# The last norm of a mixture-of-experts block: transposes after scaling replaced by products with a diagonal of the norm's weight, the mean by row products, and the idle products before the experts moved to rows of x

## The chip, the cores and the metric

The kernel runs on one core of one Trainium2 chip. The metric is the device time of one launch in microseconds; where several runs are given it is their median. A profile is one execution taken by the hardware profiler; its span runs from the first to the last instruction of the program, and its own time is a little longer. All numbers are float32 unless a line says otherwise.

## The reference

The reference is one layer over 625 nodes with 768 channels: a graph attention part, a linear attention part, and then a feed-forward part with two global norms and a mixture of experts. Only the last part is touched. With `x` the residual rows:

```
a = attn(ln(x));  h = layernorm_global(a + ln(x), ln1_w, ln1_b)
m = sum over the two best experts k of  vals[k] * (gelu(h @ fc_w[k] + fc_b[k]) @ proj_w[k] + proj_b[k])
out = x + layernorm_global(m + h, ln2_w, ln2_b)

layernorm_global(z, w, b) = (z - mean(z)) / sqrt(var(z, ddof=1) + 1e-12) * w + b
```

In `layernorm_global` mean and variance are taken over all 625 x 768 numbers; `w` and `b` have one number for each channel. The experts are chosen once for all nodes, from the mean of the router's scores.

## The kernel before, in words

**Layout.** The residual `xs` is held in rows: 5 tiles of 125 nodes (`TP`), 768 channels along the free axis. The feed-forward part works in channel-major tiles: 6 tiles (`NC`) of 128 channels (`P`), 625 nodes along the free axis. `hT` is the sum before the first norm, `x3` the normed input of the experts, `zT` the sum `m + h` before the last norm, all three channel-major. `bcol` holds bias and norm vectors by channel, in columns; `LN2W` and `LN2B` are the columns where the last norm's weight and bias begin.

**Order of the work.** A scheduler of the language orders each engine's instructions by data dependence and program order, except in blocks marked `manual_schedule`, where the named engines take program order. Semaphores between engines, and waits for memory that is used again, are put in by the language. SyncE's queue issues the weights' loads; GpSimd's queue issues loads that broadcast a vector to all partitions.

**Before the experts (L1058 to L1092).** `global_norm` (L1007) makes the mean and the factor of the first norm: statistics on VectorE, one product with `mean_w` (128 x 128, all 1/128, L1002) that gives the mean over partitions, and a power on GpSimd (L1019). `scale_bias` (L1024) turns them into a scale and a bias for each channel, and `x3` is written from `hT`. Beside this TensorE does nine products that nobody reads (L1064, `psidle`), of `mean_w` with 313 columns of `hT`. Then the memory of `hT` is given back (`fms.close()`), and the pool `ep` of the experts is opened in its place: weights `wq`, input sums `xt`, hidden tiles `h` and `t`, temporaries.

**The experts (L1219 to L1255).** A product of two matrices is done with seven half-size products in place of eight (`seven`, L1128): sums of quarter blocks of the weights (`quarter_sums` L1118, `last_sum` L1123) and of the inputs (`xt`, L1207 to L1211), all on VectorE, then seven products into four PSUM banks `al`, `be`, `ga`, `de`, and sums of the banks on VectorE (L1149 to L1162), with one copy on ScalarE (L1146). The loops run over two experts `k`, two groups `u0` of 6 pairs of hidden blocks, then over the hidden blocks `f` (first matrix, activation on ScalarE at L1234) and over three pairs of output blocks `c` (second matrix). An output quarter `q` is added to `zT` with the expert's gate (L1248); in the last group each finished half tile of `zT` is measured as well (L1251, into `st2`).

**The tail (L1262 to L1279).** `global_norm` and `scale_bias` run again for the last norm. Then `zT` is scaled in place, three channel tiles on ScalarE (L1266) and three on VectorE (L1269). For each of the five row tiles, six transposes (L1274) bring it into two PSUM banks, one VectorE add (L1277) adds `xs`, and two stores on SyncE's queue (`move_rows`, L73: rows 0 to 111 and 112 to 124) write it out. Three buffers `fin` are in use.

Of the kernel before, what the change touches and what calls it, by code (L numbers as in the profile page):

```python
# [8 lines left out]
F32 = mybir.dt.float32  # L9
# [4 lines left out]
AF = mybir.ActivationFunctionType  # L14
OP = mybir.AluOpType
# [24 lines left out]
def kernel(ctx: ExitStack, tc: tile.TileContext, a: dict, out: bass.AP):  # L40
# [1020 lines left out]
        nc.tensor.matmul(ps_r[0:1, 0:NEXP], chan[:, k, 0:1], rww[:, k, :], start=(k == 0), stop=(k == NC - 1))  # L1061

    ps_w = b1("psidle")
    for i in range(9):  # L1064
        nc.tensor.matmul(ps_w[:, 0:NH2], mean_w, hT[:, i % NC, 0:NH2], start=True, stop=True)
    att.close()


# [27 lines left out]
    pse_.close()  # L1096
    moe = ExitStack()
    ep = moe.enter_context(tc.tile_pool(name="ep", bufs=1, reuse_waits="tile"))
    psq = moe.enter_context(tc.tile_pool(name="psq", bufs=8, space=PSUM, reuse_waits="tile"))

# [22 lines left out]

    A11, A12, S1, A22, S2, S3, S4 = range(7)

    def seven(name, ws, b):  # L1128


        def product(ps, s, blk, first):
            n = 3 * len(ws)
            for k in range(n):
                nc.tensor.matmul(ps[:, 0:NH2], ws[k // 3][:, s, k % 3, :], b[blk](k),  # L1134
                                 start=(first and k == 0), stop=(k == n - 1), skip_group_check=True)

        def bank(nm):
            return psq.tile([P, BANK], F32, tag="q", name=f"{nm}_{name}")

        def tmp(nm):  # L1140
            return ep.tile([P, NH2], F32, tag=nm, name=f"{nm}_{name}", bufs=2)

        al, be, ga, de = bank("al"), bank("be"), bank("ga"), bank("de")
        product(al, A11, "11", True)
        p1 = tmp("p1")
        nc.scalar.copy(p1, al[:, 0:NH2])  # L1146
        product(be, S2, "t2", True)
        u = tmp("u")
        nc.vector.tensor_add(u, be[:, 0:NH2], p1)  # L1149
        product(ga, S1, "t1", True)  # L1150
        p5 = tmp("p5")
        nc.vector.tensor_add(p5, ga[:, 0:NH2], u)
        product(de, S3, "t3", True)
        c22 = tmp("c22")
        nc.vector.tensor_sub(c22, de[:, 0:NH2], p5)  # L1155
        product(al, A12, "21", False)
        product(ga, S4, "22", False)
        c12 = tmp("c12")
        nc.vector.tensor_add(c12, ga[:, 0:NH2], u)
        product(de, A22, "t4", False)  # L1160
        c21 = tmp("c21")
        nc.vector.tensor_sub(c21, de[:, 0:NH2], u)  # L1162
        return al[:, 0:NH2], c12, c21, c22
# [10 lines left out]


    def gates():
        ones = mp.tile([1, P], F32, name="ones")
        nc.vector.memset(ones, 1.0)
        lm = mp.tile([1, 1], F32, name="lm")
        nc.vector.tensor_scalar_mul(lm, top[:, 0:1], -1.0)  # L1180
        ls = mp.tile([1, 1], F32, name="ls")
        nc.scalar.activation(lg, lg, AF.Exp, bias=lm, accum_out=ls)
        nc.scalar.activation(top[:, 0:2], top[:, 0:2], AF.Exp, bias=lm)
        nc.vector.reciprocal(ls, ls)
        nc.vector.tensor_scalar_mul(top[:, 0:2], top[:, 0:2], ls)
        ps = psq.tile([P, BANK], F32, tag="q", name="pstv")
        nc.tensor.matmul(ps[:, 0:2], ones, top[:, 0:2], start=True, stop=True)
        vals = mp.tile([P, 2], F32, name="vals")
        nc.vector.tensor_copy(vals, ps[:, 0:2])
        ebc = []  # L1190
        for k in range(2):
            er = mp.tile([NF + NC, P], F32, tag="er", name=f"er{k}", bufs=2)
            nc.sync.dma_start(er[0:NF, :], a["L0_ffn_fc_b"][bass.ds(ex[k], 1), :].rearrange("e (f p) -> (e f) p", p=P))
            nc.sync.dma_start(er[NF:, :], a["L0_ffn_proj_b"][bass.ds(ex[k], 1), :].rearrange("e (f p) -> (e f) p", p=P))
            ps = psq.tile([P, BANK], F32, tag="q", name=f"pser{k}")
            nc.tensor.transpose(ps[:, 0:NF + NC], er, ident[0:NF + NC, 0:NF + NC])
            ec = mp.tile([P, NF + NC], F32, tag="ec", name=f"ec{k}", bufs=2)
            nc.vector.tensor_copy(ec, ps[:, 0:NF + NC])
            ebc.append(ec)
        pbias = mp.tile([P, NC], F32, name="pbias")  # L1200
        nc.vector.tensor_scalar_mul(pbias, ebc[0][:, NF:], vals[:, 0:1])
        nc.vector.scalar_tensor_tensor(pbias, ebc[1][:, NF:], vals[:, 1:2], pbias, op0=OP.mult, op1=OP.add)
        return vals, ebc, pbias
# [12 lines left out]
          "t3": lambda k: xt[:, 2, k, :], "t4": lambda k: xt[:, 3, k, :]}  # L1216

    st2 = const.tile([P, 2 * NC, 6], F32, name="st2")
    GU = 6  # L1219
    for k in range(2):  # L1220
        prw = a["L0_ffn_proj_w"][bass.ds(ex[k], 1), :, :].rearrange("e (f p) c -> p (e f) c", p=P)
        for u0 in range(0, HF, GU):
            hb = []
            for f in range(u0, u0 + GU):
                w, w_next = w_next or fc_weights(k, f), None
                cs = seven(f"f{k}_{f}", [w], bx)
                if k == 0 and f == 0:
                    vals, ebc, pbias = gates()
                    for c in range(NC):
                        nc.scalar.activation(zT[:, c, :], x3[:, c, 0:N], AF.Identity, bias=pbias[:, c:c + 1])  # L1230
                h = [ep.tile([P, NH2], F32, tag=f"h{q}", name=f"h{q}_{k}_{f}", bufs=GU + 2) for q in range(4)]
                for q in range(4):
                    fb = f + HF * (q // 2)
                    nc.scalar.activation(h[q], cs[q], AF.Gelu_apprx_tanh, bias=ebc[k][:, fb:fb + 1])  # L1234
                t = [ep.tile([P, NH2], F32, tag=f"t{q}", name=f"t{q}_{k}_{f}", bufs=GU + 2) for q in (1, 2, 4)]
                b_side(*h, t[0], t[1], h[1], t[2])
                hb.append(dict(zip(("11", "t3", "21", "22", "t1", "t2", "t4"), h + t)))
            bh = {q: (lambda i, q=q: hb[i][q]) for q in hb[0]}
            for c in range(3):
                ws = []  # L1240
                for g in range(GU // 3):
                    f = u0 + 3 * g
                    ws.append(load_quarters(f"wp{k}_{u0}_{c}_{g}", lambda i, j: prw[:, f + HF * j:f + HF * j + 3, (c + 3 * i) * P:(c + 3 * i + 1) * P]))
                cs = seven(f"p{k}_{u0}_{c}", ws, bh)
                for q in range(4):
                    cc = c + 3 * (q // 2)
                    lo, hi = (0, NH2) if q % 2 == 0 else (NH2, N)
                    nc.vector.scalar_tensor_tensor(zT[:, cc, lo:hi], cs[q][:, 0:hi - lo], vals[:, k:k + 1],  # L1248
                                                   zT[:, cc, lo:hi], op0=OP.mult, op1=OP.add)
                    if k == 1 and u0 + GU == HF:  # L1250
                        nc.vector.bn_stats(st2[:, 2 * cc + q % 2, :], zT[:, cc, lo:hi])  # L1251
                if k == 1 and u0 + GU == HF and c == 0:
                    shift = small.tile([P, 2], F32, tag="gmv", name="gmv_z")
                    nc.vector.bn_aggr(shift, st2[:, 0:2, :].rearrange("p a b -> p (a b)"))
                    shift = all_mean(shift, 2, "z", lambda nm: psq.tile([P, BANK], F32, tag="q", name=nm))[:, 0:1]  # L1255
    moe.close()
    pse_ = ctx.enter_context(ExitStack())
    psm = pse_.enter_context(tc.tile_pool(name="psm2", bufs=3, space=PSUM, reuse_waits="tile"))
    psb = pse_.enter_context(tc.tile_pool(name="psb2", bufs=2, space=PSUM, reuse_waits="tile"))


    gm, gr = global_norm(st2, shift, LN2W, LN2B, float(N * D), "n2")  # L1262
    gsc, gbi = scale_bias(gm, gr, LN2W, LN2B, "n2")
    for c in range(NC):
        if c % 2 == 0:
            nc.scalar.activation(zT[:, c, :], zT[:, c, :], AF.Identity, bias=gbi[:, c:c + 1],  # L1266
                                 scale=gsc[:, c:c + 1])
        else:
            nc.vector.tensor_scalar(zT[:, c, :], zT[:, c, :], gsc[:, c:c + 1], gbi[:, c:c + 1],  # L1269
                                    op0=OP.mult, op1=OP.add)  # L1270
    for t in range(NT):
        ps = mm(f"psz{t}").rearrange("p (b n) -> p b n", b=2)
        for c in range(NC):
            nc.tensor.transpose(ps[0:TP, c // 3, (c % 3) * P:(c % 3 + 1) * P], zT[:, c, t * TP:(t + 1) * TP],  # L1274
                                ident)
        ot = mp.tile([TP, D], F32, tag="fin", name=f"fin{t}", bufs=3)
        nc.vector.tensor_add(ot.rearrange("p (b n) -> p b n", b=2), ps[0:TP, :, 0:HALF],  # L1277
                             xs[:, t, :].rearrange("p (b n) -> p b n", b=2))
        move_rows(nc.sync, out[t * TP:(t + 1) * TP, :], ot)  # L1279


# [29 lines left out]
```

## Time and profile before

| what | value |
|---|---|
| median of three runs | 1350.59 us (1350.17 to 1351.14) |
| time of the profiled execution | 1350.35 us |
| its span | 1348.6 us |
| granted TensorE clock, mean | 0.994 |
| ScalarE busy | 273.3 us |
| GpSimd busy | 57.9 us |
| last VectorE instruction ends | 1343.79 us |

Times in the profile are microseconds from the start of the span. A row of the timeline gives start, busy time, engine, line, operation, what is written and read, shapes and count, and in brackets how long the engine stood idle before it and what released it. A row of groups gives a line's busy time, the mean duration of one instruction in ns, and the idle time before. PE is TensorE's matmul, PEld its weight load, DVE VectorE, ACT ScalarE, POOL GpSimd, SP SyncE; a q after the name is the engine's queue for issuing. Matmuls are pipelined, so starts follow each other faster than one lasts. A float32 product appears as two matmuls, a transpose as one.

### The profile page before, as it was taken

The numbers are of one execution on the slowest core, as the hardware profiler recorded it, in microseconds if no ns is written. First come the engines' busy times: TensorE is split into PE (matmuls) and PEld (weight loads), VectorE is DVE, ScalarE is ACT, GpSimd is POOL, SyncE is SP. The second block draws the span as 40 slices with busy tenths as digits, with TensorE's granted clock in tenths as the row PEclk, the third lists the DMA queues.
The fourth block names the chain that finished last, engine by engine and source line by source line (L and its number), as shares of the span: only waits on it lengthen the run. The fifth ranks groups of instructions, "written<-read, shape, count | busy, mean of one in ns | idle before, by whom it ended". The sixth has DMA issues, their size and how long they took to land.

```text
span 1348.6 us, 14927 instructions
## 1 busy us (share of the span) xinstructions
PE 1307.5 (97%) x5316; PEld 915.2 (68%) x5316; DVE 768.4 (57%) x2007; ACT 273.3 (20%) x548; POOL 57.9 (4%) x121
## 2 busy tenths in 40 slices
PE   5999999999999999999999989999999999999995
PEld 4776677655777796555665767777777777777774
DVE  5798697867575674675431376434544554445444
ACT  2121222005556471001011013100210021012100
POOL 3000110110000000000000000000000000000000
PEclk9999999999999999999999999999999999999998
DMA  7344243333112321103213132222213221322111
GB/s 221 114 129 132 63 114 81 95 102 105 62 65 73 108 101 36 35 2 127 70 36 108 54 105 69 62 78 86 71 47 93 71 71 47 94 71 71 47 47 58
DMA packets 123514, 108.63 MB, mean 81 GB/s; under 512 B 8842, under 2 KB 115072, under 8 KB 123436
## 3 DMA queue, kind: packets, MB, share of 16 engines
q1 hardware_dynamic: 114792, 86.11, 21.3%
q0 software_dynamic: 8304, 21.03, 5.1%
q8 instruction: 44, 0.72, 0.2%
q10 hardware_dynamic: 340, 0.50, 0.2%
q14 instruction: 34, 0.28, 0.1%
HBM read 103.62 MB, written 3.96 MB: 80 GB/s over the span
## 4 chain that ended last, share of the span: by engine, by line
PE 49%; issue 43%; DVE 3%; DMA 2%; ACT 2%; POOL 0%; SPq 0%; POOLq 0%; DVEq 0%; ACTq 0%
PE psq L353 6%; PE psg L662 6%; PE cnt L257 3%; PE m_o L757 3%; PE pspr L701 3%; PE psw L1045 3%; PE psx L353 3%; PE psvt L101 2%; PE m_qk L757 2%; PE psh L559 2%; PE pso L559 2%; PE alh L582 2%; PE gah L582 1%; PE deh L582 1%; PE psqk L559 1%
## 5 line engine op out<-in xcount | busy, mean ns | idle before, releaser
L353 PE MATMUL psq<-xnT,wqkv 128*128 128x313 f32 (+1 forms) x432 | 121.8, 431 | 0.0
L662 PE MATMUL psg<-h,pt 125*125 125x193 f32 x600 | 101.2, 327 | 0.3 <-ACT node L667 0.3
L662 PEld LDWEIGHTS psg<-h,pt 125*125 125x125 f32 x600 | 98.5, 188 | 4.1 <-ACT node L667 0.6
L353 PEld LDWEIGHTS psq<-xnT,wqkv 128*128 128x128 f32 x432 | 79.0, 190 | 29.1
L1134 PE MATMUL al_f<-x,wf 128*128 128x313 f32 x288 | 84.0, 427 | 0.5 <-ACT p_f L1146 0.5
L1134 PE MATMUL de_f<-xt,wf 128*128 128x313 f32 x288 | 83.8, 426 | 0.0
L1134 PE MATMUL al_p<-h,wp 128*128 128x313 f32 x288 | 79.8, 427 | 0.0
L249 DVE TENSOR_SCALAR os<-iota,src_f 125x625 f16<-125x625 f16 x165 | 63.8, 387 | 21.6 <-PE cnt L257 21.6
L1234 ACT ACTIVATE h<-c_f,ec 128x313 f32<-128x313 f32 x72 | 39.9, 557 | 176.9 <-DVE c_f L1155 109.1
L1134 PEld LDWEIGHTS al_f<-x,wf 128*128 128x128 f32 x288 | 54.3, 189 | 22.1 <-ACT p_f L1146 1.0
L1134 PEld LDWEIGHTS de_f<-xt,wf 128*128 128x128 f32 x288 | 54.5, 189 | 21.5
L1134 PEld LDWEIGHTS al_p<-h,wp 128*128 128x128 f32 x288 | 54.7, 190 | 20.9
L257 PE MATMUL cnt<-os,od 125*125 125x512 f16 (+1 forms) x418 | 66.5, 301 | 1.4 <-DVE od L255 1.4
L257 PEld LDWEIGHTS <-od 125*125 125x125 f16 x418 | 44.3, 137 | 25.5 <-DVE od L255 3.4
L643 DVE SCALAR_TENSOR_TENSOR pt<-rb,as,u 125x625 f32<-125x625 f32 x60 | 51.1, 865 | 14.7 <-ACT u L637 14.4
L255 DVE TENSOR_SCALAR od<-iota,dst_f 125x125 f16<-125x125 f16 x209 | 50.3, 254 | 13.1 <-PE cnt L257 12.8
L648 DVE SCALAR_TENSOR_TENSOR pt<-pt,AT 125x625 f32<-125x625 f32 x60 | 48.5, 808 | 8.3 <-ACT pt L646 8.1
L448 DVE CUSTOM_DVE_ANT_0 jm<-row,maskb 125x625 bf16<-125x625 f32 x60 | 48.7, 812 | 3.5 <-DMA row<-row_d 2.1
L637 ACT ACTIVATE u<-rb,asd 125x625 f32<-125x625 f32 x60 | 48.6, 811 | 0.1
L646 ACT ACTIVATE pt<-pt 125x625 f32<-125x625 f32 x60 | 43.4, 723 | 10.0 <-DVE pt L643 9.5
L342 DVE CUSTOM_DVE_ANT_0 jk<-wal,ab 128x192 f32<-128x192 f32 x144 | 41.7, 356 | 4.7 <-DMA ab<-in_L_gnn_a_dst_dram 2.7
L1134 PE MATMUL be_f<-xt,wf 128*128 128x313 f32 x144 | 42.1, 427 | 1.3 <-DVE wf L1121 1.3
(377 smaller groups left out, 2123.9 us busy)
## 6 DMA issues: line engine op xcount, KB each, us to landing
wf<-in_L_ffn_fc_w_dram SPq DMA_DIRECT2D x96, 192.0 KB
wp<-in_L_ffn_proj_w_dram SPq DMA_DIRECT2D x96, 192.0 KB
row<-row_d POOLq DMA_DIRECT2D x24, 305.2 KB, 3.7
rb<-rT_d POOLq DMA_DIRECT2D x12, 610.4 KB, 8.2
wal<-in_L_gnn_W_dram SPq DMA_DIRECT2D x18, 384.0 KB
wqkv<-in_L_mix_w_qkv_dram SPq DMA_DIRECT2D x18, 384.0 KB
wg<-in_L_gnn_W_dram SPq DMA_DIRECT2D x6, 1152.0 KB
wout<-in_L_gnn_W_out_dram SPq DMA_DIRECT2D x6, 1152.0 KB
```

The source lines that it names most:

```text
L249: nc.vector.tensor_scalar(os_, iota, src_f[:, j:j + 1], None, op0=OP.is_equal)
L255: nc.vector.tensor_scalar(od_, iota[:, b * TP:(b + 1) * TP], dst[:, j:j + 1], None, op0=OP.is_equal)
L257: nc.tensor.matmul(ps[0:TP, lo:hi], od_, os_[:, lo:hi], start=first, stop=last)
L353: nc.tensor.matmul(ps[:, 0:hi - lo], w[:, k, c0:c0 + P], xnT[:, k, lo:hi], start=(k == 0), stop=(k == NC - 1))
L448: nc.vector.tensor_tensor_reduce(jk, row, maskb[:, i, :], 1.0, -3e38, OP.add, OP.max, mx[:, i, p:p + 1])
L559: nc.tensor.matmul(ps[0:TP, 0:HALF], src[:, k, t * TP:(t + 1) * TP], w[:, k, :], start=(first and k == 0), stop=(last and k == NC - 1))
L582: nc.tensor.matmul(ps, st(k), mv(k), start=(first and k == 0), stop=(k == 2), skip_group_check=True)
L637: nc.scalar.activation(u1, rb[:, 0, :], AF.Identity, bias=asd[:, t, p:p + 1])
L643: nc.vector.scalar_tensor_tensor(pt, rb[:, 1, :], as02[:, t, p:p + 1], u1, op0=OP.add, op1=OP.max)
L662: nc.tensor.matmul(ps[0:TP, 0:GC + 1], pts[s][:, i * TP:(i + 1) * TP], hs[u, s][0][:, hd, :], start=(s == 0), stop=(s == NT - 1))
L757: nc.tensor.matmul(ps, st(sa, k, i), mv(sb, k), start=(first and k == 0), stop=(k == 2), skip_group_check=True)
L1134: nc.tensor.matmul(ps[:, 0:NH2], ws[k // 3][:, s, k % 3, :], b[blk](k), start=(first and k == 0), stop=(k == n - 1), skip_group_check=True)
```

## The change

It has four parts.

1. The idle products read `xs` in place of `hT`, and there are six of them.
2. In the middle of the first expert's first matrix (`f == 4`) a new function `tail_ready` prepares the tail: six diagonal matrices `dg` of the last norm's weight, the negated weight as a row on one partition (`nlw`, twice in a row so that 512 columns can be cut from it at any place), the norm's bias broadcast and added to `xs`, and the negated gate `nvals`.
3. For the last pair of output blocks, `seven` no longer forms `c21 = de - u`; `u` is added to `zT` with the negated gate when it is ready, and `de` straight from PSUM with the gate.
4. The tail no longer scales `zT`. Each of the 30 pieces (125 nodes x 128 channels) is multiplied with the diagonal of its channels, which turns it to rows and applies the weight at once; four pieces lie in one PSUM bank, in the order of the output. A product of the mean's row (one partition, 125 numbers) with up to 512 columns of the negated weight is added to each bank. VectorE then does one operation for each of the eight banks: bank times the norm's factor plus `xs`, which already holds the bias. TensorE's order is written out by hand: 16 pieces (the first 11 do not need the last pair of output blocks), the mean over partitions, 6 pieces, then row products with two pieces between the first four. Stores go out in halves of 384 columns, on the queues of SyncE and ScalarE.

The pool `psq` of PSUM banks now lives to the end. The diff, cut to its core:

```diff
-    for i in range(9):
-        nc.tensor.matmul(ps_w[:, 0:NH2], mean_w, hT[:, i % NC, 0:NH2], start=True, stop=True)
+    for i in range(6):
+        nc.tensor.matmul(ps_w[:, 0:NH2], mean_w[0:TP], xs[:, i % NT, 0:NH2], start=True, stop=True)
...
         product(de, A22, "t4", False)
+        if parts:
+            return al[:, 0:NH2], c12, (de[:, 0:NH2], u), c22
         c21 = tmp("c21")
...
+    def tail_ready():
+        for c in range(NC):
+            nc.vector.tensor_scalar_mul(dg[:, c, :], ident, bcol[:, LN2W + c:LN2W + c + 1])
+        for i in range(2):
+            nc.gpsimd.dma_start(nlw[:, i, :], a["L0_ffn_ln2_w"].rearrange("(o d) -> o d", o=1))
+        nc.vector.tensor_scalar_mul(nlw, nlw, -1.0)
+        lnb = bcast_row(mp, a["L0_ffn_ln2_b"], "lnb")
+        for t in range(NT):
+            nc.vector.tensor_add(xs[:, t, :], xs[:, t, :], lnb[0:TP])
+        nc.vector.tensor_scalar_mul(nvals, vals[:, 1:2], -1.0)
...
+                if k == 0 and f == 4:
+                    tail_ready()
...
+                if last and c == 2:
+                    zc = zT[:, c + 3, 0:NH2]
+                    nc.vector.scalar_tensor_tensor(zc, cs[2][1], nvals, zc, op0=OP.mult, op1=OP.add)
+                    for q, v in ((3, cs[3]), (0, cs[0]), (1, cs[1]), (2, cs[2][0])):
+                        add(q, v, vals[:, k:k + 1])
...
-    gm, gr = global_norm(st2, shift, LN2W, LN2B, float(N * D), "n2")
-    gsc, gbi = scale_bias(gm, gr, LN2W, LN2B, "n2")
-    for c in range(NC):
...
-    for t in range(NT):
-        ps = mm(f"psz{t}").rearrange("p (b n) -> p b n", b=2)
-        for c in range(NC):
-            nc.tensor.transpose(ps[0:TP, c // 3, (c % 3) * P:(c % 3 + 1) * P], zT[:, c, t * TP:(t + 1) * TP],
-                                ident)
-        ot = mp.tile([TP, D], F32, tag="fin", name=f"fin{t}", bufs=3)
-        nc.vector.tensor_add(ot.rearrange("p (b n) -> p b n", b=2), ps[0:TP, :, 0:HALF],
-                             xs[:, t, :].rearrange("p (b n) -> p b n", b=2))
-        move_rows(nc.sync, out[t * TP:(t + 1) * TP, :], ot)
+    NPC = NT * NC
+    psz = [psq.tile([P, BANK], F32, tag="q", name=f"psz{i}") for i in range((NPC + 3) // 4)]
+
+    def to_rows(pieces):
+        for i in pieces:
+            t, c = divmod(i, NC)
+            nc.tensor.matmul(psz[i // 4][0:TP, (i % 4) * P:(i % 4 + 1) * P], zT[:, c, t * TP:(t + 1) * TP], dg[:, c, :],
+                             start=i not in begun, stop=False, skip_group_check=True)
+            begun.update(range(i // 4 * 4, i // 4 * 4 + 4))
...
+    with tc.manual_schedule(engines={mybir.EngineType.PE}):
+
+        early = [i for i in range(16) if i % NC not in (2, 5)]
+        to_rows(early)
+        to_rows([i for i in range(16) if i not in early])
+
+        mv = small.tile([P, 2], F32, tag="gmv", name="gmv_n2")
+        nc.vector.bn_aggr(mv, st2.rearrange("p a b -> p (a b)"))
...
+        ps = psz[-1][:, 2 * P:2 * P + 2]
+        nc.tensor.matmul(ps, mean_w, mv, start=True, stop=True)
+        am = small.tile([P, 2], F32, tag="am", name="am_n2")
+        nc.vector.tensor_copy(am, ps)
+        gm = mp.tile([1, P], F32, name="gm_row")
+        nc.vector.tensor_scalar(gm, ones, am[0:1, 0:1], shift[0:1], op0=OP.mult, op1=OP.add)
...
+        nc.gpsimd.tensor_tensor(gr, gv, mhalf[:, 0:1], OP.pow)
+        to_rows(range(16, 22))
+        for q in range(len(psz)):
+            n = min(4, NPC - 4 * q) * P
+            off = (4 * q % NC) * P
+            nc.tensor.matmul(psz[q][0:TP, 0:n], gm[0:1, 0:TP], nlwf[0:1, off:off + n], start=False, stop=True,
+                             skip_group_check=True)
+            if q < 4:
+                to_rows(range(22 + 2 * q, 24 + 2 * q))
+            cols = slice(4 * q * P, 4 * q * P + n)
+            nc.vector.scalar_tensor_tensor(fin[:, cols], psz[q][0:TP, 0:n], gr[0:TP], xsf[:, cols],
+                                           op0=OP.mult, op1=OP.add)
+            for t in range(NT):
+                if (NC * t + NC - 1) // 4 == q:
+                    for g in range(2):
+                        cols = slice(g * HALF, (g + 1) * HALF)
+                        move_rows(nc.scalar if g else nc.sync, out[t * TP:(t + 1) * TP, cols],
+                                  fin[:, t * D + g * HALF:t * D + (g + 1) * HALF])
```

## The prediction

> **What bounds the kernel now.** I read the page first, then the tail and the start of the expert stage in the order of time, then busy time by stretch, then the groups by shape.
>
> ```profile
> PE 1307.5 (97%) x5316; PEld 915.2 (68%) x5316; DVE 768.4 (57%) x2007; ACT 273.3 (20%) x548; POOL 57.9 (4%) x121
> ```
>
> TensorE is the bound. The stretches show where it is not:
>
> ```profile
> 797.50:862.00 64.50, 64.50 (x247) 46.21 (x248) 41.15 (x89) 18.17 (x34) 0.00 (x0) 1.00 0.32 92
> ...
> 862.00:1327.50 465.50, 465.50 (x1769) 335.25 (x1767) 217.08 (x442) 52.59 (x104) 0.00 (x0) 1.00 0.23 67
> ```
>
> The columns are stretch and length, then busy time of PE, PEld, DVE, ACT, POOL, then granted clock. From 797.5 to 1327.5 PE is busy without a hole at clock 1.00, DVE for under half of the long stretch. So a microsecond won before 797.5 is carried to the end, DVE work inside the stage is free while PE isn't kept waiting, and everything after 1327.5 is bare. The tail, in order of time:
>
> ```profile
> 1324.35 3.32 PE L1134 MATMUL de_p<-t,wp 128*128 128x313 f32 x12
> ...
> 1330.31 0.38 PE L1002 MATMUL psam_n<-gmv_n,mean_w 128*128 128x2 f32 x2 [2.64 <-DVE gmv_n L1013]
> ...
> 1333.70 4.20 PE L1274 MATMUL psz<-ident,zT 128*125 128x128 f32 x18 [3.00 <-ACT zT L1266]
> ...
> 1342.83 0.96 DVE L1277 TENSOR_TENSOR fin<-psz,xs 125x768 f32<-125x768 f32 x1 [0.86 <-DMA out_dram<-fin]
> ...
> 1344.18 0.39 SPq L76 DMA_DIRECT2D out_dram<-fin  x1
> ```
>
> The last product streams out at 1324.35 + 12 x 0.263 = 1327.5; 21.1 us of statistics, norm, transposes, adds and stores follow, with PE idle for most of the first six. At the start of the stage:
>
> ```profile
> 786.79 6.53 PE L1065 MATMUL psidle<-hT,mean_w 128*128 128x313 f32 x18
> ...
> 793.35 1.14 DVE L1207 TENSOR_TENSOR xt<-x 128x939 f32<-128x939 f32 x1 [2.19 <-PE psidle L1065]
> ...
> 795.58 0.55 DVE L1119 TENSOR_TENSOR wf<-wf 128x384 f32<-128x384 f32 x1
> ...
> 797.46 1.82 PE L1134 MATMUL be_f<-xt,wf 128*128 128x313 f32 x6 [1.26 <-DVE wf L1121]
> ```
>
> DVE is held 2.19 us by the idle products, since xt takes memory in which hT lies, which they read; PE then waits for the weight sums behind it.
>
> **The change part by part.** Durations are those of the profiled execution: span 1348.6, its own time 1350.35, 0.24 below the median of 1350.59; I subtract from the median.
>
> **Idle products on rows of x.** xs stays allocated, so xt no longer waits for PE. Its inputs are there at 790.8 (four DVE writes of x3 from 788.62, 2.15 us); DVE does xt and its second sum (1.14 + 1.14) by about 793.5. The next thing late is the weights: the trace's landing marks for the four quarters are 792.80, 793.60, 794.28 and 795.20, and the three sums need the first three. So the sums start at 794.3 in place of 795.58, and be_f at 796.2 in place of 797.46: 1.25 us, not the 2.19 of the wait. Six in place of nine drop six matmuls of 0.263 = 1.6 us, so PE is done at 791.6 and the first weight product waits for 792.80 (it began at 793.15). Clock: the records of the trace have it change on a grid of 3.41 us (786.48, 789.89, 1332.61, 1339.44). The next period, 789.9 to 793.3, would hold 1.7 us of idle products and 0.45 of the first product, 63%.
>
> ```profile
> 1325.95:1329.35 3.40, 1.72 (x7) 0.93 (x5) 1.72 (x5) 0.00 (x0) 0.00 (x0) 1.00 0.00 0
> ...
> 1336.17:1339.43 3.26, 3.06 (x15) 2.77 (x14) 2.35 (x3) 0.00 (x0) 0.00 (x0) 0.50 0.18 50
> 783.07:786.48 3.41, 1.22 (x9) 0.63 (x8) 1.96 (x6) 0.00 (x0) 0.00 (x0) 1.00 0.00 0
> ```
>
> A period busy for 51% kept the clock (first line), one of 36% lost it (last line). At 63% I count it as kept. If lost, PE runs half speed from 793.3 to 796.7, where it waits for most of the time anyway: 0.3 us.
>
> **Preparations in the stage (tail_ready).** On DVE: six diagonals at the 284 ns of the 128x128 scale = 1.7; the negated row of 1536, twice the 0.68 of a 768-column scale = 1.4; five adds of 125x768 at 0.95 = 4.75; together 7.9 us, in a stage where DVE has 248 us idle. On POOL's queue: three loads, where nothing else waits until the last power. The adds wait for the broadcast, whose like (384 KB) landed 4.4 to 5.5 us after issue; behind a waiting add stand DVE's PSUM sums. Cover: at 846.04 p5 is computed and its bank is needed again by PE at 848.29, a slack of 1.8 us after its 0.48. Pieces of at most 1.4 us between PSUM reads cost nothing; all in one block costs 7.9 - 1.8 = 6.1. No gain is possible. I take 0, as the present weight sums slip between the PSUM sums one at a time.
>
> **Last product split.** c21 (0.48 at 1327.71) leaves the chain; the other half is done earlier, in DVE's idle time. The statistics come 0.5 us sooner. Worth nothing by itself, because PE is busy with pieces then.
>
> **To rows, norm and mean.** Removed behind 1327.5: three scale operations (1331.97 to 1332.71), three ACT and three DVE passes over zT, 30 transposes, five adds. Added on PE: 30 products with a diagonal, 8 row products, in one order with the mean.
>
> ```profile
> L915 PE MATMUL pss<-qk_rows 125*128 125x128 f32 x60 | 8.0, 277 | 0.0
> ...
> L1274 PE MATMUL psz<-ident,zT 128*125 128x128 f32 x30 | 6.4, 397 | 3.2 <-ACT zT L1266 3.0 <-DVE fin L1277 0.2
> ...
> L943 PE MATMUL psoa<-vT,scT 128*128 128x512 f32 x12 | 6.3, 605 | 0.2 <-DVE ot L945 0.2
> ```
>
> Each f32 product is two matmuls, a transpose one. The starts of L915's follow each other at 0.112 us, of L943's 512-column ones at 0.43, both at full clock. PE: 60 x 0.112 = 6.7; seven rows x 2 x 0.43 = 6.0; the 256-column row 0.43; the mean 0.4 (1330.31 to 1330.73): 13.6 us. It doesn't wait in between: the first 16 pieces take 3.6 us, the statistics 2.3; six pieces (1.3 us) stand behind the mean, while the mean's row takes about 0.6; the power's chain (am at 1330.73 to gr at 1331.96, 1.23 us, plus 0.2 for the row) ends as row product 0 begins. What a row product of one partition costs no large row shows; the nearest are 256 ns for the 1*128 product of the gates against 262 for the 128-row mean, both of two columns, so I price by columns. Below: 0.25 us each if one-row products were free of streaming, for which nothing speaks; above: twice as much at half clock, taken up under the rivals.
>
> The Trainium skill speaks against this (TensorE: Matmul & The Clock Gate, Terms): transpose mode is four times faster for FP32. By the rule, transposes at full clock would take 6.7 / 4 = 1.7 us, and products lose 5.0. In the trace transposes start every 0.213 us at half clock and every 0.11 once it is full (from 1339.49): 3.3 us for 30, a factor of two. So against warm transposes the change pays 3.4, but those of before ran nearly all at clock 0.50. The page's Part 4 has transposes not engaging the full clock; here it rose at 1339.44 after a period with nothing else. I use the measured 0.112 and full clock, since PE never rests now.
>
> DVE: eight scale-and-adds. A 312-column one from PSUM took 0.54, one of 939 columns 1.14; hence 0.75 for 512 and 0.49 for 256, under PE's 0.86 a bank. PE ends at 1327.5 + 13.6 = 1341.1; bank 6 is seen at 1340.8, DVE ends 1340.8 + 0.75 + 0.04 + 0.49 = 1342.1, against 1343.79: 1.7 us.
>
> **Stores.** Twenty in place of ten, ten each on SP's and ACT's queues; ACT's issue of x took 0.33 and 0.41, like SP's 0.35 and 0.39, and ACT has no other work. From the last add to the end it is 1348.6 - 1343.8 = 4.8 us. Two issues per queue remain behind the last add, so I keep 4.8. The data would allow it: 0.38 MB at 290 GB/s are 1.3 us; rows 4 follow rows 2 and 3, whose banks come at about 1339.9 and 1340.7, and end near 1344.6, no later than by the 4.8. Half-width rows may cost up to 0.5 or gain 0.5.
>
> Sum: 1.25 + 1.7 = 2.9; 1350.6 - 2.9 = 1347.7.
>
> **Rivals.** (1) The weight or clock takes back the start: only the tail gains, 1348.9 to 1349.3. For it: 1.25 us hangs on landings; against: the marks are clear. (2) The clock falls in the tail, because row products with one active row count as idle. Shifted by 1.25, PE's part runs from 1326.25 to 1339.8; the period 1332.6 to 1336.0 holds only 34% diagonal products, below the 36% that lost it. The remaining 3.8 us double: 1351.5. For it: that threshold; against: nothing shows that rows matter. (3) Slower: DVE's preparations stand in one block in front of p5 or c22 and PE waits for its bank. The price is the block less 1.8 us; it turns the sum from a block of 4.7 us on, and the whole 7.9 gives 1347.7 + 6.1 = 1353.8, more if the broadcast's landing is waited for. For it: five adds with one wait; against: DVE's idle half. (4) The change doing nothing: PE in the tail merely exchanges idle for work and DVE ends where it did; it would take 1.7 us more on PE, 1349.3, in the same band as (1).
>
> **How the numbers follow.** A difference of 0.2% (2.7 us) is about what a measurement of this kernel can tell from no change: below 1347.9 is faster, above 1353.3 slower. Forecast 0.59, with its own range 1346.3 to 1348.9: 0.40 faster, 0.19 same. Rivals (1) and (4) together 0.14: same. (2) 0.13: 0.08 same, 0.05 slower if it also meets a shifted period. (3) 0.14: 0.04 same, 0.10 slower. So faster 0.40, same 0.45, slower 0.15. The range is 1346.3 to 1352.6: it takes in (1), (2) and the smaller half of (3).
>
> **What would show it.** xt beginning near 791 and be_f near 796.2; no PE hole near the fifth expert block; in the tail, matmul starts 0.112 and 0.43 apart at clock 1.00, 13.6 us from the last product to the last row product, DVE following each row by 0.2 us, and 4.8 us from the last add to the end. The prediction is wrong if the clock column shows 0.50 in the tail, if DVE waits stand before PE around the preparations, or if stores last longer.

## The result, and the profile after

The changed kernel takes 1357.62 us (median of 6 runs, 1354.78 to 1361.48) against 1350.59 before (also six runs): ratio 1.0052, 95% interval 1.0039 to 1.0065. It is slower by 7 us, where 2.9 us less were forecast, and outside the range. The profiled execution took 1357.78 with a span of 1356.0, 7.4 above that of before. Three differences make up the 7.4: the last expert product begins at 1329.23 in place of 1324.35 (4.9 later); from there to the end of VectorE's last operation (1352.40) it is 23.2 us in place of 19.4 (3.7 more); from that operation to the end 3.6 in place of 4.8 (1.2 less).

```profile
1329.23 3.32 PE L1134 MATMUL de_p<-t,wp 128*128 128x313 f32 x12
...
1351.07 1.33 DVE L1338 SCALAR_TENSOR_TENSOR fin<-psz,gr_n,xs 125x512 f32<-125x512 f32 x2 [0.96 <-PE psz L1333]
```

The start of the expert stage after the change, in order of time; the first two rows are preparations that `tail_ready` makes:

```profile
759.18 1.13 DVE L1229 TENSOR_SCALAR dg<-ident,bcol 128x128 f32<-128x128 f32 x6
...
762.85 0.93 DVE L1232 TENSOR_SCALAR nlw<-nlw 1x1536 f32<-1x1536 f32 x1
...
787.17 6.40 PE L1065 MATMUL psidle<-xs,mean_w 125*128 125x313 f32 x12
...
789.66 0.96 DVE L1235 TENSOR_TENSOR xs<-xs,lnb 125x768 f32<-125x768 f32 x1 [0.92 <-PE psidle L1065]
...
790.61 0.15 DVE L1078 FIND_INDEX8 tix<-top,lg 1x8 uint32<-1x8 f32 x1
...
790.81 0.94 DVE L1235 TENSOR_TENSOR xs<-xs,lnb 125x768 f32<-125x768 f32 x1
...
792.36 2.18 SPq L1112 DMA_DIRECT2D wf<-in_L_ffn_fc_w_dram  x4
...
795.11 1.82 PE L1134 MATMUL al_f<-x,wf 128*128 128x313 f32 x6 [1.54 <-DMA wf<-in_L_ffn_fc_w_dram]
...
798.69 0.94 DVE L1235 TENSOR_TENSOR xs<-xs,lnb 125x768 f32<-125x768 f32 x1
...
800.25 3.40 PE L1134 MATMUL be_f<-xt,wf 128*128 128x313 f32 x6 [3.32 <-DVE wf L1121]
```

Two rows of before for comparison:

```profile
788.49 0.15 DVE L1078 FIND_INDEX8 tix<-top,lg 1x8 uint32<-1x8 f32 x1
...
790.24 2.18 SPq L1112 DMA_DIRECT2D wf<-in_L_ffn_fc_w_dram  x4
```

Look at L1235, the addition of the norm's bias to `xs`. It is written into the fifth expert block, but stands between the router's instructions, 60 us earlier. The first one waits 0.92 us for the idle products, which read `xs`, and lasts 0.96. Behind it stands the search for the experts' index, which starts at 790.61 where it started at 788.49 before. The issue of the weights' loads follows the index (792.36 now, 790.24 before). Of the other four additions one follows the index, one stands in front of `xt`, and two stand between the weight sums. So `be_f` comes at 800.25 in place of 797.46, and runs at half speed: 3.40 us in place of 1.82.

The clock in these stretches (length, busy times of PE, PEld, DVE, ACT, POOL, then the granted clock, DMA's share and GB/s). As in before, the clock changes on a grid of 3.41 us; a step of it is called a period here:

```profile
786.37:789.79 3.42, 3.42 (x19) 2.58 (x20) 1.52 (x11) 0.00 (x0) 0.56 (x1) 0.50 0.00 0
796.60:800.02 3.42, 0.33 (x2) 0.00 (x0) 3.42 (x6) 1.70 (x2) 0.00 (x0) 1.00 0.61 174
800.02:803.44 3.42, 3.19 (x6) 2.19 (x7) 2.64 (x4) 0.00 (x0) 0.00 (x0) 0.50 0.93 263
1335.92:1339.33 3.41, 3.41 (x23) 2.41 (x22) 1.36 (x5) 0.00 (x0) 0.55 (x1) 1.00 0.00 0
1339.33:1342.74 3.41, 3.41 (x13) 1.65 (x14) 1.62 (x3) 0.00 (x0) 0.00 (x0) 1.00 0.36 111
1342.74:1348.00 5.26, 5.26 (x9) 2.22 (x9) 1.14 (x3) 0.00 (x0) 0.00 (x0) 0.50 0.37 112
```

The second line is the period in which TensorE waited for the held-up sums (0.33 us busy); the third, at clock 0.50, is its price. The last three lines are the tail: in 1339.33 to 1342.74 TensorE is busy without a hole, and the clock falls to 0.50 at its end all the same. The tail's rows:

```profile
1337.52 1.12 PE L1333 MATMUL psz<-nlw,gm_row 1*125 1x512 f32 x2
1338.56 0.51 PEld L1300 LDWEIGHTS psz<-dg,zT 128*125 128x125 f32 x4 [0.76 <-issue]
1338.56 0.70 PE L1300 MATMUL psz<-dg,zT 128*125 128x128 f32 x4
...
1339.19 1.12 PE L1333 MATMUL psz<-nlw,gm_row 1*125 1x512 f32 x2
...
1345.55 6.33 PE L1333 MATMUL psz<-nlw,gm_row 1*125 1x512 f32 x8
```

A row product and two pieces take 1339.19 - 1337.52 = 1.67 us, with the weight loads of the pieces standing idle for 0.76; 1.31 were forecast. The last eight matmuls, four row products, take 6.33 at half clock.

### The profile page after: what moved, and what is told of

Read it like the earlier page. It is cut to its first block, busy times and chain, and to the rows that moved or that the text cites. A ratio compares the mean times of both kernels' runs of the same rounds, so it can differ in the third digit from the quotient of the medians.

```text
span 1356.0 us, 15032 instructions
## 1 busy us (share of the span) xinstructions
PE 1320.7 (97%) x5356; PEld 919.9 (68%) x5356; DVE 772.9 (57%) x2017; ACT 270.8 (20%) x545; POOL 59.9 (4%) x124
## 4 chain that ended last, share of the span: by engine, by line
PE 88%; DVE 4%; issue 3%; ACT 2%; DMA 2%; POOL 0%; ACTq 0%; DVEq 0%; SPq 0%; POOLq 0%
PE psq L353 6%; PE de_f L1134 6%; PE ga_f L1134 6%; PE al_p L1134 6%; PE de_p L1134 6%; PE ga_p L1134 6%; PE al_f L1134 5%; PE psg L662 5%; PE cnt L257 3%; PE m_o L757 3%; PE be_f L1134 3%; PE pspr L701 3%; PE psw L1045 3%; PE be_p L1134 3%; PE psx L353 3%
## 5 line engine op out<-in xcount | busy, mean ns | idle before, releaser
L255 DVE TENSOR_SCALAR od<-iota,dst_f 125x125 f16<-125x125 f16 x209 | 49.7, 251 | 13.2 <-PE cnt L257 12.9
```

What stands on the lines that cost most here:

```text
L255: nc.vector.tensor_scalar(od_, iota[:, b * TP:(b + 1) * TP], dst[:, j:j + 1], None, op0=OP.is_equal)
```

## The experiments

Theory A for the start: the additions are placed by the scheduler as early as their data allows; free, they would have gone before the router, but the idle products on xs must read it first, so they fell in between, into the router's chain. Rivals: six idle products are too few for the clock (B), or the preparations as a whole cost the time (C). Theory D for the tail: a product of one partition (one row of the array) counts as idle for the clock, and TensorE drains between one-row and full products. Rival E: rows don't matter, the clock fell for another reason.

**a_hT9**: the changed kernel with the idle products of before.

```diff
-    for i in range(6):
-        nc.tensor.matmul(ps_w[:, 0:NH2], mean_w[0:TP], xs[:, i % NT, 0:NH2], start=True, stop=True)
+    for i in range(9):
+        nc.tensor.matmul(ps_w[:, 0:NH2], mean_w, hT[:, i % NC, 0:NH2], start=True, stop=True)
```

> The changed kernel with the old nine idle products on hT; all else of the change stays. Theory A (the five adds of the norm's bias into xs were held back by the idle products that read xs, and so fell into the router's chain on VectorE): with xs free, the adds move to before the router, be_f starts near 797.5 as before, and only the tail's loss of about 2.5 us is left: 1353 us. Theory B (the start was lost because six idle products are too few to hold the clock) also gives 1353, but with the adds still between the router's instructions. Theory C (the start was lost by the preparations as a whole): stays near 1357.

Measured: 1355.44 us, ratio 1.0039 (1.0028 to 1.0050). The group of the additions, with first and last start:

```profile
L1235 DVE TENSOR_TENSOR xs<-xs,lnb x5: 895/936/940, 763.4 to 768.6; 125x768 f32<-125x768 f32 x5
```

They moved some 20 us ahead of the router, and `be_f` starts at 797.08, about as before. That settles where they fall. It speaks against C, but only by the trace: the interval of the time overlaps that of the changed kernel. The time is 2 us more than expected. The trace shows 0.9 of a new wait, of a product that gives a mean over partitions before the router, behind the additions on VectorE:

```profile
PE psam_half L1002 <- DVE gmv_half L1055: 0.9, 1, 0.9
```

The rest is not placed. The profiled execution took 1353.33, near the fastest of the 15 (1352.87 to 1359.85), and its clock was 1.00 through the whole start, where that of before was 0.50 from 786.48 to 789.89. Slower executions may have lost the clock; none of them has a trace.

**a_hT6**: as a_hT9, but six products on hT.

```diff
-        nc.tensor.matmul(ps_w[:, 0:NH2], mean_w[0:TP], xs[:, i % NT, 0:NH2], start=True, stop=True)
+        nc.tensor.matmul(ps_w[:, 0:NH2], mean_w, hT[:, i % NC, 0:NH2], start=True, stop=True)
```

> The changed kernel with six idle products, but on hT. Parts count from operand: if the operand xs alone lost the start (it chains the adds behind the idle products), the adds go before the router as with nine on hT, where they cost 0.9 us, and xt waits little: 1353 to 1354 us. If the count of six lost it, the time stays near 1357.

Measured: 1354.39 us, ratio 1.0029 (1.0019 to 1.0039), nearer to the theory of the operand than to 1357. The additions again stand at 763.7 to 768.8. The profiled execution is the slowest of its runs (1358.82): the clock was 0.50 from 793.65 to 803.89, after TensorE had stood idle 2.8 us for the first weights. With nine products such slow executions occur as well (four of the 15 of a_hT9 took over 1357.5, two of the 10 here), so it is not shown that the count brings them about; the intervals of six and nine overlap.

**a_pin**: the changed kernel, six products on xs, the additions tied to the fifth block.

```diff
+        one = mp.tile([P, 1], F32, name="one")
+        nc.vector.tensor_scalar(one, cs[2][:, 0:1], 0.0, 1.0, op0=OP.mult, op1=OP.add)
...
-            nc.vector.tensor_add(xs[:, t, :], xs[:, t, :], lnb[0:TP])
+            nc.vector.scalar_tensor_tensor(xs[:, t, :], lnb[0:TP], one[0:TP], xs[:, t, :], op0=OP.mult, op1=OP.add)
```

> The changed kernel with its six idle products on xs, and the five adds tied to a result of the fifth expert block by a factor of one, so that they can't come earlier. Theory A: the start is even 1.25 us better than before, be_f near 796.2, and with the tail's loss of 2.5 us the time is near 1352; if the five adds in one block hold a PSUM bank, up to 3 us more. Theory B: the start stays as late as in the changed kernel, 1357.

Measured: 1352.28 us, ratio 1.0016 (1.0009 to 1.0024), as theory A has it. The start and the additions in its timeline:

```profile
791.19 1.14 DVE L1207 TENSOR_TENSOR xt<-x 128x939 f32<-128x939 f32 x1
...
793.36 1.82 PE L1134 MATMUL al_f<-x,wf 128*128 128x313 f32 x6 [1.19 <-DMA wf<-in_L_ffn_fc_w_dram]
...
796.32 1.75 PE L1134 MATMUL be_f<-xt,wf 128*128 128x313 f32 x6
...
852.46 4.74 DVE L1237 SCALAR_TENSOR_TENSOR xs<-lnb,one,xs 125x768 f32<-125x768 f32 x5
```

`be_f` comes at 796.32, forecast 796.2. The five additions stand in one block of 4.74 us, and TensorE waits for no other engine from 850 to the tail. From 1.0052 to 1.0016: the misplaced additions cost about 5 us, give or take 2 by the two intervals, some two thirds of the loss. The gain of the idle products, which they took away, is in it. Theory B had 1357 for this kernel, which has six products too: it falls as the main cause.

**b_idle**: the kernel before, with the six products on xs alone (the edit of the idle products in the change).

> The kernel before with only the six idle products on xs; tail and preparations untouched. Theory A: xt no longer waits, be_f near 796.2, 1349.3 us. Theory B: the clock falls at the start, 1351 us or more.

Measured: 1349.04 us, ratio 0.9988 (0.9981 to 0.9995); `be_f` starts at 795.66 in this trace. This part of the change is a gain of 1.6 us, forecast 1.25.

**a_pin128**: a_pin with the row products over all 128 partitions; `nlw` and `ones` get 128 partitions too.

```diff
-            nc.gpsimd.dma_start(nlw[:, i, :], a["L0_ffn_ln2_w"].rearrange("(o d) -> o d", o=1))
-        nc.vector.tensor_scalar_mul(nlw, nlw, -1.0)
+            nc.gpsimd.dma_start(nlw[:, i, :], a["L0_ffn_ln2_w"].partition_broadcast(P))
+        nc.vector.tensor_scalar_mul(nlw, nlw, -1.0 / P)
...
-        gm = mp.tile([1, P], F32, name="gm_row")
-        nc.vector.tensor_scalar(gm, ones, am[0:1, 0:1], shift[0:1], op0=OP.mult, op1=OP.add)
+        gm = mp.tile([P, P], F32, name="gm_row")
+        nc.vector.tensor_scalar(gm, ones, am[:, 0:1], shift, op0=OP.mult, op1=OP.add)
...
-            nc.tensor.matmul(psz[q][0:TP, 0:n], gm[0:1, 0:TP], nlwf[0:1, off:off + n], start=False, stop=True,
+            nc.tensor.matmul(psz[q][0:TP, 0:n], gm[:, 0:TP], nlwf[:, off:off + n], start=False, stop=True,
```

> a_pin with the row products over 128 partitions: the mean on all partitions, the negated weight broadcast and divided by 128; same sum, same columns. Theory D (a product of one partition counts as idle for the clock, and TensorE drains when it changes between one-row and full products): clock 1.00 to the end, a row product and two pieces in 1.31 us in place of 1.67, 4 to 5 us less than a_pin: near 1348. Rival E (columns streamed under any number of rows set clock and time, and the clock fell for another reason): as a_pin, within 1 us.

Measured: 1348.63 us, ratio 0.9984 (0.9977 to 0.9991). Its tail in order of time:

```profile
1332.84 1.02 PE L1335 MATMUL psz<-nlw,gm_row 128*125 128x512 f32 x2
1333.27 0.19 PEld L1302 LDWEIGHTS psz<-dg,zT 128*125 128x125 f32 x1 [0.24 <-issue]
1333.70 0.60 PE L1302 MATMUL psz<-dg,zT 128*125 128x128 f32 x4
...
1334.13 1.02 PE L1335 MATMUL psz<-nlw,gm_row 128*125 128x512 f32 x2
...
1338.02 3.17 PE L1335 MATMUL psz<-nlw,gm_row 128*125 128x512 f32 x8
...
1339.08 2.86 DVE L1340 SCALAR_TENSOR_TENSOR fin<-psz,gr_n,xs 125x512 f32<-125x512 f32 x4 [0.54 <-PE psz L1335]
```

The clock, by period, in a_pin, with one row:

```profile
1333.07:1336.48 3.41, 3.41 (x13) 1.60 (x12) 1.50 (x2) 0.00 (x0) 0.00 (x0) 1.00 0.19 56
1336.48:1339.90 3.42, 3.42 (x7) 1.41 (x6) 0.75 (x1) 0.00 (x0) 0.00 (x0) 0.50 0.55 168
```

The same two periods in a_pin128:

```profile
1333.07:1336.48 3.41, 3.41 (x16) 2.00 (x15) 1.50 (x2) 0.00 (x0) 0.04 (x1) 1.00 0.19 56
1336.48:1339.90 3.42, 3.42 (x15) 1.97 (x14) 2.25 (x3) 0.00 (x0) 0.00 (x0) 1.00 0.66 197
```

The same columns, the same sum, TensorE without a hole in both: with one row the clock falls at 1336.48, with 128 it stays. A row product and two pieces take 1.29 us. From the end of the last expert product's stream (1327.8) to that of the last row product TensorE needs 13.2 us, forecast 13.6; in a_pin it needed 20. Both effects of theory D go with the number of rows, and E falls; that TensorE "drains" between the forms is an image, which no run tests.

This execution shows another thing. Its clock was 1.00 when the idle products began, so they were over at 790.4, and TensorE stood idle 2.86 us for the first weights. Three periods from its start:

```profile
785.80:789.21 3.41, 2.94 (x23) 2.30 (x24) 2.45 (x17) 0.46 (x1) 0.56 (x1) 1.00 0.00 0
789.21:792.63 3.42, 1.18 (x5) 0.53 (x3) 3.42 (x8) 1.72 (x5) 0.00 (x0) 1.00 0.26 70
792.63:796.04 3.41, 2.79 (x6) 1.84 (x6) 2.47 (x5) 0.00 (x0) 0.00 (x0) 0.50 0.62 177
```

After a period busy for 1.18 us, 35%, the clock fell, and `be_f` came at 797.59, no earlier than before. What this execution gained (span 1346.9 against 1348.6), it gained in the tail.

**a_pin_last**: a_pin, one-row products again, all pieces ahead of them.

```diff
-        to_rows(range(16, 22))
+        to_rows(range(16, NPC))
...
-            if q < 4:
-                to_rows(range(22 + 2 * q, 24 + 2 * q))
```

> a_pin with all 30 pieces ahead of the row products, which stay on one partition. Theory D: no change between one-row and full products in the middle, 4 x 0.38 = 1.5 us less; the clock still falls, at the end of the first period of 3.41 us that holds mostly row products, though TensorE is never idle; TensorE's part 14.6 to 18 us in place of 20: near 1349. Rival E (the order doesn't matter, row products are as good as any for the clock): 1352 as a_pin.

Measured: 1350.05 us, ratio 0.9991 (0.9983 to 0.9998). By the ratios, each to the runs of before beside it, that is 3.4 us below a_pin; about 3 were expected. Its clock by period:

```profile
1332.09:1335.50 3.41, 3.41 (x22) 2.55 (x22) 0.30 (x1) 0.00 (x0) 0.30 (x1) 1.00 0.00 0
1335.50:1338.92 3.42, 3.42 (x10) 1.45 (x9) 3.06 (x5) 0.00 (x0) 0.00 (x0) 1.00 0.48 142
1338.92:1341.90 2.98, 2.98 (x6) 1.06 (x4) 1.57 (x3) 0.00 (x0) 0.00 (x0) 0.50 0.84 266
```

The middle period holds nothing but one-row products; the clock falls at its end, with TensorE busy throughout and no change of form in it. That excludes hidden gaps at such changes as the whole reason. In the first period 1.9 us, a little over half, went to pieces, which are full products, and the clock was kept. The loss is smaller since there is no change between the forms to pay for, and more of the work is done when the clock falls.

**a_pin128_9**: a_pin128 with nine idle products on xs.

```diff
-    for i in range(6):
+    for i in range(9):
```

> a_pin128 with nine idle products on xs in place of six. In the profile of a_pin128 the clock fell at 792.6 after a gap of 2.9 us; nine close that gap, but at half clock they last 9.5 us and then hold up the first weights. If the gap is what costs, 1347.5 with a narrower spread; if late ends weigh more, 1349 to 1350 with a wider one.

Measured: 1349.15 us, ratio 0.9980 (0.9971 to 0.9989). Neither expectation is shown: by the ratios it can't be told from a_pin128. Six or nine idle products made no difference that these runs can tell, here or between a_hT6 and a_hT9.

**a_pin128_bf**: a_pin128 with the mean's row and the weight in it rounded to bf16, which changes that one term of the sum.

```diff
+    nlwb = mp.tile([P, 2, D], BF16, name="nlwb")
...
-        gm = mp.tile([P, P], F32, name="gm_row")
+        gm = mp.tile([P, P], BF16, name="gm_row")
```

> a_pin128 with the row products in bf16 (mean and weight of that one term rounded to bf16): one matmul of about 0.215 us in place of two of 0.43. TensorE's part 13.6 to 8.8 us; VectorE is then the bound, 6 us from the factor at 5.6, so its last operation comes 2.7 us sooner; the stores, 1.9 MB at 290 GB/s, may take back up to 0.5: 1346.3 us. If rows were not the tail's limit, 1348.6 as a_pin128.

Measured: 1345.34 us (4 runs, 1345.19 to 1346.96), ratio 0.9956 (0.9939 to 0.9972). It is faster than the kernel before and than a_pin128, though four runs are few. Its first two row products, and VectorE's eight operations:

```profile
1333.32 0.38 PE L1336 MATMUL psz<-nlwb,gm_row 128*125 128x512 bf16 x1
...
1333.81 5.09 DVE L1341 SCALAR_TENSOR_TENSOR fin<-psz,gr_n,xs 125x512 f32<-125x512 f32 x8 [0.84 <-PE psz L1336]
...
1333.97 0.38 PE L1336 MATMUL psz<-nlwb,gm_row 128*125 128x512 bf16 x1
```

A row product and two pieces take 0.65 us here, and VectorE goes through its banks in one block: the row products had been the tail's limit. VectorE ends at 1338.9, and from there to the span's end (1345.2) it is 6.3 us, where a_pin128 has 5.0. So the stores are probably late next; the traced execution is the slowest of the four (1346.96), and no run takes this further.

## Why the prediction was wrong, point by point

**The idle products on xs.** Right in mechanism and near in size when alone (b_idle: 1.6 us, forecast 1.25). Wrong in company: the prediction asked who waits for hT, and did not ask who writes xs next. The part that frees one wait made another, 0.92 us before 789.66.

**Preparations in the stage, taken as 0.** This is the step that failed first. It assumed that tail_ready's instructions run where they are written, at the fifth block, and put its price on a held PSUM bank there. After the change the diagonals stand at 759, the negated row at 763 and the additions from 789.7 to 799.6. The queue in front of which they stood was the router's. a_pin shows that in the place assumed the additions cost nothing, and that the place they took cost about 5 us. The third rival had the engine and the sign, but named the wrong instructions behind the block (`p5` and `c22`), and its price was for another place. For that place the price is not tested; by the same slack of 1.8 us the block of 4.74 in a_pin would have cost 2.9, and TensorE didn't wait for it.

**Row products priced by columns.** The second step that failed. The sum of 13.6 us for TensorE is met when the rows are full (13.2 in a_pin128); with one row the columns stream as fast (0.43 us for 512 in a_pin_last, at full clock), but each change to the pieces and back takes 0.38 us more (1.67 against 1.29), and the clock falls. The row taken for the price, 256 ns for a 1*128 product of two columns, shows one product alone, neither a change between forms nor a period's clock. The second rival had the mechanism: 3.8 us of TensorE's time doubled was its price. From a_pin to a_pin128 the ratio falls from 1.0016 to 0.9984, 4.3 us, give or take 1.4, clock and changes together. The rival was held at 0.13 because nothing showed that rows matter; neither did anything show that they don't.

**The clock at the start, counted as kept at 63%.** Kept in b_idle and a_pin, in periods busy for 70 and 65%. But the 63% assumed that the idle products run at half clock at first. Where the clock was full when they ran (a_pin128, a_hT6), they were over sooner, the period was busy for only 35 and 38%, and the clock fell. The term held by luck of the grid, and the first rival had its failure: the clock takes back the start. In after it fell at 800.02, as a consequence of the late sums. There it had also risen one period late: the idle products began at 787.17 in a period from 786.37, filled 77% of it, and the clock stayed at 0.50, where 91% had been enough before (small products fill the rest, so the busy column is full in both). The grid's place differs from run to run, and part of the spread may come from it. One reading was off the grid: the stretch said to be busy for 51% begins 0.17 us late; on the grid, 1325.78 to 1329.20, it is 1.89 of 3.42 us, 55%.

**The split of the last product; VectorE's eight operations; the stores.** Right: 0.75 us for 512 columns as forecast, VectorE behind TensorE all the way. In after it is 3.6 us from VectorE's last operation to the end, probably since the late tail had let earlier rows leave; in a_pin128, 5.0 against the 4.8 forecast.

With both failed steps mended (a_pin128) the change gains 0.16% of 1350.6, 2.2 us (1.2 to 3.1); the forecast sum was 2.9.

## What to carry to other kernels

Work prepared ahead ran where the scheduler found its operands free, not where it stood in the source: for each such instruction ask who last reads what it writes, and what on its engine then stands behind it. A dummy operation that reads a live buffer is a reader like any other. And a product's price has three parts, its stream, its change from the form before it, and what it does to the clock: where a one-row product can be spread over all partitions at the same number of columns, try that; here it gave back the 4.3 us.

## What the runs showed of the hardware

One-row float32 products did not hold TensorE's clock: with the engine busy for a whole period of 3.41 us, the clock fell to 0.50 in after, a_pin and a_pin_last, while the same columns under 128 rows kept it. That is shown. That they count as nothing fits, but was not measured by itself. Periods with idle time kept the clock when busy for 55% (before, from 1325.78; after, from 793.20) and lost it at 35 to 38% (a_pin128, before, a_hT6); counting full products alone, the tail's periods were kept at 55% (a_pin_last, 1.9 us of pieces) and lost at 37% (after and a_pin, 0.63 us of pieces in each 1.68). Nor is it shown why a change between the two forms and back costs 0.38 us. In after the pieces' weight loads stand idle for 0.76 us and begin with the pieces themselves (both at 1338.56), where in a_pin128 the first load begins 0.43 us ahead (1333.27 and 1333.70), as if weights could not be brought in under a one-row product.
